# Reordered steps in a transformer kernel's second attention, and the spill slots' downward product joined with the next upward one

## The chip, the cores and the metric

The kernel runs on one core of one Trainium2 chip. The metric is the time on the device in microseconds (us), from the start of the launch to its end. A core has five engines that run side by side, each from a stream of instructions of its own: TensorE (PE in the profile, with its weight loads as PEld) multiplies matrices and transposes through an identity matrix, VectorE (DVE) works elementwise and along rows, ScalarE (ACT) applies functions such as the exponential, GpSimd (POOL) does general elementwise work and indirect transfers, and SyncE (SP) issues plain DMA transfers. An engine takes its instructions strictly in the order in which they were written to it; where one needs another engine's result, it waits on a semaphore, and everything behind it on that engine waits too. Matmul results go to PSUM, from which VectorE or ScalarE must copy them; operands of matmuls lie in SBUF.

## The reference

The input is `x [8, 256, 256]` (8 batches, 256 tokens, width 256) and a context of the same shape, in f32. Four residual stages follow one another, each on the layer norm of `x`:

```python
x = x + L0_xattn(layernorm(x), ctx, ctx)   # autocorrelation attention by FFT, top-12 shifts
x = x + L0_ffn(layernorm(x))               # 8 experts, balanced assignment, gelu
x = x + L1_xattn(layernorm(x), ctx)        # the attention of this document
x = x + L1_ffn(layernorm(x))               # the mixture of this document
```

The change touches the last two only. Cut to what matters:

```python
def L1_xattn(x, data):            # 16 heads of width 16
    q = (x @ Wq + bq).reshape(bs, n_ctx, 16, 16)
    kv = (data @ Wkv + bkv).reshape(bs, n_data, 16, 32)
    k, v = kv[..., :16], kv[..., 16:]
    attn = softmax(einsum('bqhd,bkhd->bhqk', q, k) / sqrt(16))
    return einsum('bhqk,bkhd->bqhd', attn, v).reshape(...) @ Wp + bp

def L1_ffn(x):                    # 8 routed experts, 8 shared slices
    probs = softmax(flat @ gate_W.T)
    top_v, top_i = top_k(probs, 2)           # two experts per token
    out_e = einsum('etf,efd->etd', silu(flat @ w1_e) * (flat @ w3_e), w2_e)
    routed = einsum('te,etd->td', gates, out_e)
    shared = einsum(..., silu(x @ w1_s) * (x @ w3_s), w2_s) / 8
    return 0.5 * shared + 0.5 * routed
```

## The kernel before

**Order.** The whole program is under a manual schedule: the order in which the Python code issues instructions is the order on each engine. Nothing plans or moves work afterwards. Work that is to overlap is therefore written between other work, with generators that are advanced step by step (`next`).

**Stages.** The first two residual stages end at some 217 us. The second attention runs from 217 to 349 us, the shared slices' first blocks around 349 to 397 us, and the blocks of the mixture to the end at 824 us.

**The attention** is a loop over 8 batches `b` and, inside, 2 halves `c` of 8 heads each (line 2968 onward). One iteration (b,c) issues, in this order: `scores(b,c,0)` for the first 128 keys (four matmuls that fill two PSUM tiles, then two exponentials `ex` on ScalarE; the pool of score tiles has two, so the next scores need both read); the values of the previous iteration (`values`, 16 matmuls with 32-wide weights) and their copy `ov` out of PSUM on VectorE (`keep`); one `send`; one step of the router; then a turning step that depends on c. With c = 0, `turn_q(b+1)` transposes the next batch's normalised tokens on TensorE into one PSUM tile and VectorE copies them to `hT`. With c = 1, `turn_out(b-1)` transposes the previous batch's attention output `on`, VectorE copies it to `oT`, and `norm_q(b+2)` with `add_bias(b+2)` normalise a later batch and add the output bias to it. Then come `scores(b,c,1)`, and behind them further router steps, the mixture's statistics for batch b-2 (`batch_stats` on VectorE and POOL, then `norm_m`, two normalisations on POOL that write into the row table `HP`), one more `send`, and the rest, by the half of the iteration: with c = 0 `turn_back` (transposes of `ov`, reciprocal sums `rs` and division into `on`), `queries(b+1, 0)` and `(b+1, 1)`; with c = 1 `turn_m` (mixture tokens transposed into `HT`), `project_out` (the product with Wp, added to X).

`queries` makes one PSUM tile `pp` of two matmuls and reads it twice into the masked `QM`: ScalarE writes the part m = 0, VectorE the part m = 1. These PSUM tiles, like those of the transposes and of the router, come from one pool, `ps_m`, with three buffers that go round in the order of allocation.

Batch 1 is an exception: in iteration (0,1) `turn_q(1)`, `norm_q(2)` and both `queries(1, ...)` all stand ahead of `scores(0,1,1)`. Batch 0 is another: ahead of the loop, `transpose_tokens` (line 1238) takes two PSUM tiles, one for each half of the width; VectorE copies the first and ScalarE the second.

**The router** (`route(g)`, for four tiles of 128 tokens, begun at b = 4 and b = 6) is a generator of eight steps: logits `pl` and their copy `lT`; their transpose `pt`, the row maximum and the exponential; two steps that pick the best and the second expert and end in the mask `mk`; the counting matmuls `pc` and the gates into `HP`; the running row numbers `run`, which read `pc`; the row numbers `to`. Each row tile is then sent by an indirect DMA of POOL (`send`) to the table `Td` in DRAM, ordered by expert.

**The mixture** works through 11 blocks: two of shared slices, eight experts (b = 2 to 9) and a last shared one. An expert's block is four upward units k = 0 to 3 and, between k = 0 and k = 1, the downward unit of the block before; a unit is a series of seven matrix products with 128-wide weights (recombined as in Strassen's method). Rows that an expert has above its fixed capacity go into four spill slots of 32 rows, whose experts are known only at run time. The generator `slots` handles them in quarters q of the hidden width, with the slots' weights loaded by SP at run-time addresses: `load_slots(q)` issues twelve DMAs of 256 KB (eight `sab` for w1 and w3, four `sc` for w2) into one buffer each. A quarter has three steps: up (`pgu`, 16 matmuls with 32-wide weights, then silu and product into `a`), turn (`a` transposed into `aT`), down (`pys`, 8 matmuls, 32 wide, followed by the loads of the next quarter). The block loop advances the generator by one step behind each unit k = 1 to 3. The quarters' steps stand at (3,1) to (6,3), so that one quarter goes with each of the blocks 3 to 6. The last step scales the sum into `Ys` and adds its rows to the output by indirect DMAs of POOL.

Of the kernel before, what the change touches and what calls it, by code (L numbers as in the profile page):

```python
# [19 lines left out]
P = 128  # L20
# [1066 lines left out]
def fast_path(  # L1087
# [1502 lines left out]
    def norm_q(b, *engs):  # L2590
        h2s[b] = hn.tile([P, TPB, D], F32, tag="h4", name="h2")
        batch_norm(b, "q", h2s[b], engs)
# [8 lines left out]
    def turn_pair(src, dst, copy):  # L2601
# [5 lines left out]
                )  # L2607
        copy(dst, pt.rearrange("p k j q -> p k (j q)"))

    def turn_q(b):  # L2610
        hTs[b] = pq2.tile([P, KC, S], F32, tag="hT", name="hT")
        turn_pair(h2s.pop(b), hTs[b], nc.vector.tensor_copy)

    def queries(b, c):
        if c == 0:
            QM[b] = pq2.tile([P, NB, 2, S], F32, tag="QM", name="QM")
        pp = ps_m.tile([P, S], F32, tag="pm", name="pp")
        for kc in range(KC):
            nc.tensor.matmul(  # L2619
                pp,  # L2620
                wq[:, kc, c * P : (c + 1) * P],
                hTs[b][:, kc, :],
                start=(kc == 0),
                stop=(kc == KC - 1),
            )
        nc.scalar.activation(
            QM[b][:, c, 0, :],
            pp,
            AF.Identity,
            bias=bqm[:, c, 0:1],  # L2630
            scale=mask[:, 0:1],
        )
        nc.vector.tensor_scalar(
            QM[b][:, c, 1, :],
            pp,
            mask[:, 1:2],
            bqm[:, c, 1:2],
            ALU.mult,
            ALU.add,
        )  # L2640

    pex = at.enter_context(tc.tile_pool(name="pex", bufs=4))
    ex, pvs, ovs, ons, oTs = {}, {}, {}, {}, {}
# [305 lines left out]
        list(vals(i, 2, ps_m))  # L2949
    norm_q(0, nc.vector, nc.vector)  # L2950
    hTs[0] = pq2.tile([P, KC, S], F32, tag="hT", name="hT")
    transpose_tokens(h2s[0], hTs[0], ps_m, "pm", 0)
    nc.vector.tensor_tensor(bpb, bpb, pbp, ALU.add)
    queries(0, 0)
    queries(0, 1)
# [12 lines left out]
    for b in range(B):  # L2968
        for c in range(NB):
            scores(b, c, 0)  # L2970
            if (b, c) == (3, 0):
                router_weights()
            if prev:
                values(*prev, 0)
                values(*prev, 1)
                keep(*prev)
            send()
            if gates:
                next(gates, None)
            if prev is None:  # L2980
                list(vals(4, 1, ps_m, nc.vector.tensor_copy))
            elif b == 0:
                turn_q(1)
                norm_q(2, nc.vector, nc.vector)
                queries(1, 0)
                queries(1, 1)
            elif c == 0:
                if b + 1 < B:
                    turn_q(b + 1)
            else:  # L2990
                turn_out(b - 1)
                if 2 < b + 2 < B:
                    norm_q(b + 2, nc.vector, nc.vector if b < 2 else nc.gpsimd)
                    add_bias(b + 2)
            scores(b, c, 1)
            if gates:
                next(gates, None)
            if c == 0 and b >= 2:
                batch_stats(b - 2, "m")
                norm_m(b - 2)  # L3000
            send()
            if gates:
                next(gates, None)
            if c == 0:
                if b >= 1:
                    turn_back(b - 1)
                if 0 < b and b + 1 < B:
                    queries(b + 1, 0)
                    queries(b + 1, 1)
                if b + 2 < B and b:  # L3010
                    add_y(b + 2)
                    batch_stats(b + 2, "q")
                if b >= 4 and b % 2 == 0:
                    gates = route(b // 2 - 2)
                    next(gates)
            else:
                if b >= 2:
                    turn_m(b - 2)
                if b >= 1:
                    project_out(b - 1)  # L3020
                else:
                    add_bias(2)
            if prev is None:
                list(vals(5, 1, ps_m, nc.vector.tensor_copy))
                ct_scope.close()
                wsp = ctx.enter_context(tc.tile_pool(name="wsp", bufs=1, side="right"))
                pg1 = ctx.enter_context(tc.tile_pool(name="pg1", bufs=1, side="right"))
# [12 lines left out]
                idx = pg1.tile([P, GT, E], F32, name="idx")  # L3040
                tri = pg1.tile([P, P], BF16, name="tri")
                ones_b = pg1.tile([P, P], BF16, name="ones_b")
                ends = pg1.tile([P, E], F32, name="ends")
                place_i = pg1.tile([P, 1], I32, name="place_i")
                slot = pg1.tile([P, 1], F32, name="slot")
                none = pg1.tile([P, 1], F32, name="none")
                bases = [
                    pg1.tile([P, E], F32, name=f"base{g}") for g in range(NT // GT + 1)
                ]
                nc.sync.dma_start(out=gw, in_=L1_ffn_gate_W)  # L3050
                WS = load_l1(wsp, -1)
            if (b, c) == (1, 0):
                router_columns()
            prev = b, c
# [4 lines left out]
    NQ = 4  # L3059
# [537 lines left out]
            for g in range(SLOTS)  # L3597
        ]

    def load_slots(q):  # L3600


        fs = slice(q * FQ, (q + 1) * FQ)
        wab = wsp.tile([P, 2, SLOTS, KC, FQ], F32, tag="wab", name=f"sab_{q}")
        wc = wsp.tile([P, SLOTS, FQ // P, D], F32, tag="wc", name=f"sc_{q}")
        wa, wb = wab[:, 0], wab[:, 1]
        for w, src in ((wa, L1_ffn_w1_e), (wb, L1_ffn_w3_e), (wc, L1_ffn_w2_e)):
            for g, e in enumerate(experts):
                part = src[bass.ds(e, 1)]
                part = part[:, fs, :] if w is wc else part[:, :, fs]  # L3610
                nc.sync.dma_start(
                    out=w[:, g], in_=part.rearrange("o (c p) d -> p (o c) d", p=P)
                )
        return wa, wb, wc

    def slots():

# [5 lines left out]
            in_=Td,  # L3623
            in_offset=bass.IndirectOffsetOnAxis(ap=rows_u, axis=0),
        )
        w = load_slots(0)
        yield
        gate = pg1.tile([P, 1], F32, name="gate")
        junk = pg1.tile([P, E], F32, name="junk")
# [14 lines left out]
        nc.vector.tensor_copy(RT, pt)  # L3644
        yield
        py = ps_v.tile([P, D], F32, tag="pv", name="pys")
        for q in range(NQ):
            pgu = ps_m.tile([P, 2, FQ], F32, tag="pm", name="pgu")
            for i in range(2):
                for kc in range(KC):  # L3650
                    for g in range(SLOTS):
                        nc.tensor.matmul(
                            pgu[g * SR : (g + 1) * SR, i, :],
                            RT[:, kc, g * SR : (g + 1) * SR],
                            w[i][:, g, kc, :],
                            start=(kc == 0),
                            stop=(kc == KC - 1),
                            skip_group_check=True,
                        )
            a = pe2.tile([P, FQ], F32, tag="as", name="as", bufs=1)  # L3660
            nc.scalar.activation(a, pgu[:, 0, :], AF.Silu)
            nc.vector.tensor_tensor(a, a, pgu[:, 1, :], ALU.mult)
            yield
            pt = ps_m.tile([P, FQ // P, P], F32, tag="pm", name="pt")
            for fi in range(FQ // P):
                nc.tensor.transpose(pt[:, fi, :], a[:, fi * P : (fi + 1) * P], ident)
# [3 lines left out]
            for fi in range(FQ // P):  # L3670
                for g in range(SLOTS):
                    nc.tensor.matmul(
                        py[g * SR : (g + 1) * SR, :],
                        aT[:, fi, g * SR : (g + 1) * SR],
                        w[2][:, g, fi, :],
                        start=(q == 0 and fi == 0),
                        stop=(q == NQ - 1 and fi == FQ // P - 1),
                        skip_group_check=True,
                    )
            if q + 1 < NQ:  # L3680
                w = load_slots(q + 1)
            else:
                WS = load_l1(wsp, -1)
                Y = pe2.tile([P, D], F32, tag="Ys", name="Ys", bufs=1)
                nc.scalar.activation(Y, py, AF.Copy, scale=gate)
                for g in range(SLOTS):
                    add_rows(Y[g * SR : (g + 1) * SR, :], ids[:, g : g + 1])
# [252 lines left out]
```

## Time and profile before

Three runs took 821.92, 823.33 and 821.46 us, a median of 821.92. One further execution was taken by the hardware profiler; it took 825.85 us, of which 824.1 lie between its first and its last instruction (its span).

| what | before |
|---|---|
| median of the runs | 821.92 us |
| profiled execution, whole | 825.85 us |
| profiled execution, span | 824.1 us |
| instructions | 13,790 |
| mean granted TensorE clock | 0.993 of full speed |
| HBM read, written | 80.61 MB, 25.37 MB |
| DMA mean | 133 GB/s |

TensorE's share by stage, with VectorE, ScalarE and POOL beside it (busy us):

| stretch, us | length | PE | DVE | ACT | POOL | clock |
|---|---|---|---|---|---|---|
| 0 to 217 | 217 | 204.34 | 121.05 | 87.52 | 64.43 | 0.98 |
| 217 to 349 | 132 | 126.45 | 82.28 | 81.20 | 60.55 | 0.99 |
| 349 to 397 | 48 | 48.00 | 25.60 | 12.82 | 20.01 | 1.00 |
| 397 to 824 | 427 | 419.83 | 290.36 | 180.21 | 71.61 | 1.00 |

How to read it: an instruction's line number (L2619) is that of the kernel printed above. A row of a chain or of the timeline gives the start in us from the span's start, the duration, the engine, and the written tile with its line. A row of windows gives, for a stretch, its length, then busy time and number of instructions of PE, PEld, DVE, ACT and POOL, the granted clock, the share of time in which the DMA engines were busy, and GB/s. Blocks 3 to 6, each with a quarter of the slots, take 40.16 us each; those without take 36.68.

### The profile page before, as it was taken

How to read it: one execution, taken by the hardware profiler on the slowest of the kernel's cores; microseconds unless marked ns; L12 is line 12 of the kernel's file. 1: busy time of each engine (PE TensorE's matmuls, PEld its weight loads, DVE VectorE, ACT ScalarE, POOL GpSimd, SP SyncE). 2: the span in 40 equal slices, each digit the busy share in tenths (PEclk: the TensorE clock that was granted, in tenths of full speed). 3: DMA queues.
4: the chain of work that ended last, by engine and by line, in shares of the span. 5: the costliest groups of instructions: out<-in, count | busy, mean ns of one | idle time of the engine just before them, and what ended most of it. 6: DMA issues, size and time to landing. Idle time of an engine off the chain costs nothing.

```text
span 824.1 us, 13790 instructions
## 1 busy us (share of the span) xinstructions
PE 798.6 (97%) x5124; PEld 630.4 (76%) x5124; DVE 519.3 (63%) x1470; ACT 361.8 (44%) x672; POOL 216.6 (26%) x293
## 2 busy tenths in 40 slices
PE   7999999999989999999999999999999999999997
PEld 6546778778745555556899989898979798999986
DVE  6368877440356585655685868676676768586731
ACT  4334544423356666532333544444444544443330
POOL 6343122131123646462330000202020323112030
PEclk9999999999999999999999999999999999999999
DMA  8395467962160100133214395385858495411023
GB/s 261 84 296 169 146 161 214 326 217 84 52 179 14 27 2 15 41 110 135 71 42 110 81 306 161 81 274 115 252 139 282 107 301 111 154 14 20 7 36 123
DMA packets 104724, 109.59 MB, mean 133 GB/s; under 512 B 26408, under 2 KB 95240, under 8 KB 104616
## 3 DMA queue, kind: packets, MB, share of 16 engines
q1 hardware_dynamic: 95976, 95.30, 38.1%
q0 software_dynamic: 7920, 13.02, 7.6%
q8 instruction: 42, 0.69, 0.4%
q10 hardware_dynamic: 752, 0.30, 0.1%
q14 instruction: 34, 0.28, 0.1%
HBM read 80.61 MB, written 25.37 MB: 129 GB/s over the span
## 4 chain that ended last, share of the span: by engine, by line
PE 88%; DVE 4%; DMA 4%; ACT 1%; issue 1%; POOL 0%; ACTq 0%; SPq 0%; DVEq 0%; POOLq 0%
PE a L3233 18%; PE e L3233 9%; PE a L3292 9%; PE py L2389 6%; PE ph L2372 6%; PE B L3233 5%; PE e L3292 4%; PE p L2652 4%; PE pv L2669 4%; PE pgu L3195 3%; PE py L3438 3%; PE B L3292 2%; DMA R<-NMd,ids 2%; PE pp L2720 2%; PE pp L2619 2%; PE pp L1419 2%
## 5 line engine op out<-in xcount | busy, mean ns | idle before, releaser
L3536 POOL DMA_INDIRECT Od<-Y,ids x32 | 52.3, 1636 | 288.1 <-DVE Y L3361 98.6
L3221 ACT COPY B<-a 128x512 f32<-128x512 f32 (+1 forms) x54 | 28.6, 531 | 169.6 <-PE a L3233 133.6
L2660 ACT ACTIVATE ex<-p,scale 128x1024 f32<-128x1024 f32 x64 | 67.9, 1111 | 34.1 <-PE p L2652 33.3
L3233 PE MATMUL a<-T,HP 128*128 128x256 f32 x288 | 73.9, 379 | 0.0
L3233 PE MATMUL a<-RT,wab 128*128 128x256 f32 x256 | 66.7, 383 | 0.4 <-DVE cc L3083 0.4
L3083 DVE TENSOR_TENSOR cc<-e,s 128x512 f32<-128x512 f32 x44 | 30.4, 691 | 57.6 <-PE e L3233 57.5
L2372 PE MATMUL ph<-RT,w 128*128 128x256 f32 x256 | 63.3, 396 | 0.8 <-ACT RT L2359 0.7
L3083 DVE TENSOR_TENSOR act<-act 128x256 f32<-128x256 f32 (+1 forms) x120 | 61.4, 512 | 2.7
L2389 PE MATMUL py<-w,A 128*128 128x256 f32 x256 | 61.6, 388 | 0.0
L3233 PEld LDWEIGHTS a<-T,HP 128*128 128x128 f32 x288 | 54.0, 190 | 7.0
L2381 ACT ACTIVATE A<-ph,b1c 128x256 f32<-128x256 f32 x64 | 30.1, 473 | 55.5 <-PE ph L2372 48.2
L2372 PEld LDWEIGHTS ph<-RT,w 128*128 128x128 f32 x256 | 46.3, 194 | 9.2 <-ACT A L2381 1.1
L3233 PEld LDWEIGHTS a<-RT,wab 128*128 128x128 f32 x256 | 46.3, 190 | 9.2 <-DVE cc L3083 2.5
L2389 PEld LDWEIGHTS py<-w,A 128*128 128x128 f32 x256 | 46.6, 190 | 6.4
L2894 POOL DMA_INDIRECT Td<-HP,to x32 | 33.0, 1030 | 60.5 <-DMA Td<-HP,to 52.6
L2652 PE MATMUL p<-QM,KT 32*128 32x512 f32 x256 | 40.5, 640 | 1.7 <-ACT ex L2660 1.2
L3083 DVE TENSOR_TENSOR act<-act,cc 128x512 f32<-128x512 f32 x44 | 30.3, 688 | 16.9 <-ACT act L3267 16.7
L2399 POOL DMA_INDIRECT Yd<-Y,ids x16 | 15.8, 986 | 83.3 <-DVE Y L2398 48.6
L3248 ACT COPY s<-a 128x512 f32<-128x512 f32 x44 | 25.8, 587 | 20.0 <-PE a L3233 20.0
L3233 PE MATMUL e<-T,wab 128*128 128x256 f32 x128 | 32.9, 380 | 0.3 <-DVE T L3083 0.3
L3233 PE MATMUL e<-RT,HP 128*128 128x256 f32 x128 | 32.8, 379 | 0.0
L3233 PE MATMUL B<-RT,wab 128*128 128x256 f32 x128 | 32.8, 379 | 0.0
(522 smaller groups left out, 1730.4 us busy)
## 6 DMA issues: line engine op xcount, KB each, us to landing
w<-in_L_ffn_w_dram SPq DMA_DIRECT2D x16, 1024.0 KB
wab<-in_L_ffn_w_e_dram SPq DMA_DIRECT2D x16, 1024.0 KB
wc<-in_L_ffn_w_e_dram SPq DMA_DIRECT2D x8, 1024.0 KB
sab<-in_L_ffn_w_e_dram SPq DMA_DIRECT2D x32, 256.0 KB
R<-Td SPq DMA_DIRECT2D x8, 530.0 KB
sc<-in_L_ffn_w_e_dram SPq DMA_DIRECT2D x16, 256.0 KB
Td<-blank SPq DMA_DIRECT2D x2, 1590.0 KB
X<-in_x_dram SPq DMA_DIRECT2D x4, 512.0 KB
```

Of the source, the lines that this page charges most:

```text
L2372: nc.tensor.matmul(ph, w1[:, kc, f * P : (f + 1) * P], RT[:, kc, :], start=(kc == 0), stop=(kc == KC - 1),)
L2381: nc.scalar.activation(A[:, f, :], ph, AF.Gelu_apprx_tanh, bias=b1c[:, e, f : f + 1])
L2389: nc.tensor.matmul(py, A[:, f, r * P : (r + 1) * P], w2[:, f, :], start=(f == 0), stop=(f == NF - 1),)
L2652: nc.tensor.matmul(ps[g // 2][:, g % 2].rearrange("p m q -> p (m q)"), KT[rows, c, k0 : k0 + P], QM[b][rows, c].rearrange("p m q -> p (m q)"),
L2660: nc.scalar.activation(e4[:, 2 * j : 2 * j + 2], ps[j], AF.Exp, scale=scale)
L2669: nc.tensor.matmul(pvs[b, c][32 * g : 32 * g + 32, m, :], VA[:, b * TPB + kt, 8 * c + 2 * g + m, :], ex[b, c, kt][:, g, m, :], start=(kt = ...
L2894: nc.gpsimd.indirect_dma_start(out=Td, out_offset=bass.IndirectOffsetOnAxis(ap=to[g][:, k, j : j + 1], axis=0), in_=HP[:, GT * g + j, :], ...
L3083: eng.tensor_tensor(out, a, b, op)
L3221: nc.scalar.copy(self.b[:, 0 : self.n], self.a[:, 0 : self.n])
L3233: nc.tensor.matmul(ps[:, m * HT2 : (m + 1) * HT2], self.w.get(m, left, self.k), self.x.part[right], start=start and m == 0, stop=True, ski ...
L3292: nc.tensor.matmul(ps[:, qs], self.acts[k][:, left, qs], self.w.get(right, k), start=start and i == 0 and k == 0, stop=(k == NK - 1), skip ...
L3536: nc.gpsimd.indirect_dma_start(out=Od, out_offset=bass.IndirectOffsetOnAxis(ap=ids, axis=0), in_=Y, in_offset=None, compute_op=ALU.add,)
```

## The change

It moves work between places of these two stages and changes the engine of two copies and of two masked products; the matmuls are the same in kind and number.

1. In iteration (0,1), both `queries(1, ...)` and `norm_q(2)` go from ahead of `scores(0,1,1)` to behind them (and behind the iteration's second `send`), the queries now ahead of `norm_q(2)`. For these queries both masked products are VectorE's (`eng=nc.vector`); for the other batches they stay split between ScalarE and VectorE.
2. Batch 0 is transposed by `turn_pair` into one PSUM tile, and two VectorE copies (`in_two`) take it to `hT`.
3. The mixture's statistics and `norm_m(b-2)` go from behind `scores(b,0,1)` to directly behind `scores(b,0,0)`, that is, ahead of the previous iteration's values, of `ov` and of `send`.
4. The first router step of an iteration goes behind `turn_q` or `turn_out`; `norm_q(b+2)` and `add_bias(b+2)` go behind that router step.
5. `load_slots` is split into upward and downward weights. A slots' step now holds the down product of quarter q and directly behind it the up product of quarter q+1; the turn stays a step of its own. The downward weights of q+1 are loaded behind the down product of q, the upward weights of q+2 behind the up product of q+1. The steps stand at (3,1) to (5,3): up 0; turn 0; down 0 and up 1; turn 1; down 1 and up 2; turn 2; down 2 and up 3; turn 3; down 3 with the additions.

```diff
+    def in_two(dst, src):
+        for kc in range(KC):
+            nc.vector.tensor_copy(dst[:, kc], src[:, kc])
+
-    def queries(b, c):
+    def queries(b, c, eng=nc.scalar):
...
+        for m in range(2):
+            if m == 0 and eng is nc.scalar:
+                nc.scalar.activation(
+                    QM[b][:, c, m, :],
+                    pp,
+                    AF.Identity,
+                    bias=bqm[:, c, m : m + 1],
+                    scale=mask[:, m : m + 1],
+                )
+            else:
+                nc.vector.tensor_scalar(
+                    QM[b][:, c, m, :],
+                    pp,
+                    mask[:, m : m + 1],
+                    bqm[:, c, m : m + 1],
+                    ALU.mult,
+                    ALU.add,
+                )
...
-    transpose_tokens(h2s[0], hTs[0], ps_m, "pm", 0)
+    turn_pair(h2s[0], hTs[0], in_two)
...
             scores(b, c, 0)
+            if c == 0 and b >= 2:
+                batch_stats(b - 2, "m")
+                norm_m(b - 2)
             if (b, c) == (3, 0):
                 router_weights()
...
             send()
-            if gates:
-                next(gates, None)
             if prev is None:
                 list(vals(4, 1, ps_m, nc.vector.tensor_copy))
             elif b == 0:
                 turn_q(1)
-                norm_q(2, nc.vector, nc.vector)
-                queries(1, 0)
-                queries(1, 1)
             elif c == 0:
                 if b + 1 < B:
                     turn_q(b + 1)
             else:
                 turn_out(b - 1)
-                if 2 < b + 2 < B:
-                    norm_q(b + 2, nc.vector, nc.vector if b < 2 else nc.gpsimd)
-                    add_bias(b + 2)
+            if gates:
+                next(gates, None)
+            if c == 1 and 2 < b + 2 < B:
+                norm_q(b + 2, nc.vector, nc.vector if b < 2 else nc.gpsimd)
+                add_bias(b + 2)
             scores(b, c, 1)
             if gates:
                 next(gates, None)
-            if c == 0 and b >= 2:
-                batch_stats(b - 2, "m")
-                norm_m(b - 2)
             send()
             if gates:
                 next(gates, None)
+            if (b, c) == (0, 1):
+                queries(1, 0, nc.vector)
+                queries(1, 1, nc.vector)
+                norm_q(2, nc.vector, nc.vector)
...
-    def load_slots(q):
...
+    def load_slots_up(q):
+        fs = slice(q * FQ, (q + 1) * FQ)
+        wab = wsp.tile([P, 2, SLOTS, KC, FQ], F32, tag="wab", name=f"sab_{q}")
...
+    def load_slots_down(q):
+        fs = slice(q * FQ, (q + 1) * FQ)
         wc = wsp.tile([P, SLOTS, FQ // P, D], F32, tag="wc", name=f"sc_{q}")
...
-        w = load_slots(0)
+        wab, wc = load_slots_up(0), load_slots_down(0)
         yield
...
-        for q in range(NQ):
+
+        def way_up():
             pgu = ps_m.tile([P, 2, FQ], F32, tag="pm", name="pgu")
...
-            yield
+            return a
+
+        a = way_up()
+        wab = load_slots_up(1)
+        yield
+        for q in range(NQ):
             pt = ps_m.tile([P, FQ // P, P], F32, tag="pm", name="pt")
...
             if q + 1 < NQ:
-                w = load_slots(q + 1)
+                wc = load_slots_down(q + 1)
+                a = way_up()
+                if q + 2 < NQ:
+                    wab = load_slots_up(q + 2)
             else:
                 WS = load_l1(wsp, -1)
```

More of the change, by code (lines that the diff above doesn't have):

```diff
@@ L2625, in queries @@
             )
[L2626 to L2640, printed above, removed]
+        for m in range(2):
[16 more added lines that the diff above has]
+                )
     pex = at.enter_context(tc.tile_pool(name="pex", bufs=4))
@@ L3598, in slot_experts @@
         ]
-    def load_slots(q):
+    def load_slots_up(q):
         fs = slice(q * FQ, (q + 1) * FQ)
         wab = wsp.tile([P, 2, SLOTS, KC, FQ], F32, tag="wab", name=f"sab_{q}")
-        wc = wsp.tile([P, SLOTS, FQ // P, D], F32, tag="wc", name=f"sc_{q}")
[L3606 to L3614, printed above, removed]
+        for m, src in enumerate((L1_ffn_w1_e, L1_ffn_w3_e)):
+            for g, e in enumerate(experts):
+                nc.sync.dma_start(
+                    out=wab[:, m, g],
+                    in_=src[bass.ds(e, 1)][:, :, fs].rearrange(
+                        "o (c p) d -> p (o c) d", p=P
+                    ),
+                )
+        return wab
+    def load_slots_down(q):
+        fs = slice(q * FQ, (q + 1) * FQ)
+        wc = wsp.tile([P, SLOTS, FQ // P, D], F32, tag="wc", name=f"sc_{q}")
+        for g, e in enumerate(experts):
+            nc.sync.dma_start(
+                out=wc[:, g],
+                in_=L1_ffn_w2_e[bass.ds(e, 1)][:, fs, :].rearrange(
+                    "o (c p) d -> p (o c) d", p=P
+                ),
+            )
+        return wc
     def slots():
@@ L3654, in slots @@
                             RT[:, kc, g * SR : (g + 1) * SR],
-                            w[i][:, g, kc, :],
+                            wab[:, i, g, kc, :],
                             start=(kc == 0),
@@ L3674, in slots @@
                         aT[:, fi, g * SR : (g + 1) * SR],
-                        w[2][:, g, fi, :],
+                        wc[:, g, fi, :],
                         start=(q == 0 and fi == 0),
```

## The prediction

> **What bounds the kernel now.** I read part 1 of the page first, then the chain that ended last, then that chain in order of time for the attention (217 to 349 us) and the mixture (349 to the end), and at last windows over the places where it leaves TensorE.
>
> ```profile
> PE 798.6 (97%) x5124; PEld 630.4 (76%) x5124; DVE 519.3 (63%) x1470; ACT 361.8 (44%) x672; POOL 216.6 (26%) x293
> PE 88%; DVE 4%; DMA 4%; ACT 1%; issue 1%; POOL 0%; ACTq 0%; SPq 0%; DVEq 0%; POOLq 0%
> ```
>
> TensorE is the path, so an edit pays only where PE idles, runs slow or pays for a change of shape. Over 470 us from 350 on, PE is busy 466.8, so only the attention has waits to give. In windows (us; then busy of PE, PEld, DVE, ACT, POOL; granted clock; DMA share; GB/s):
>
> ```profile
> 231.70:242.80 11.10, 9.08 (x72) 4.25 (x71) 6.28 (x14) 6.51 (x8) 5.24 (x8) 0.99 0.94 246
> 242.80:246.30 3.50, 3.50 (x35) 1.47 (x34) 0.00 (x0) 1.21 (x2) 0.00 (x0) 0.55 0.63 200
> 305.90:308.90 3.00, 1.14 (x15) 0.93 (x11) 2.66 (x14) 2.12 (x2) 1.06 (x3) 1.00 0.00 0
> ```
>
> PE loses 2.0 us before 242.8, then has half a clock, then loses 1.9 us in iteration (5,0), where VectorE is nearly full. From 246.3 to 305.9 it is busy all 59.6 us: what the change moves there is free unless it makes a wait. I write (b,c) for an iteration of the loop.
>
> **Part 1, queries of batch 1 behind the second scores of (0,1).** The chain there:
>
> ```profile
> 235.03 0.69 DVE ov L2679
> 235.72 0.61 DVE hT L2608
> ...
> 236.37 1.99 PE pp L2619 x8
> 238.37 1.08 PE p L2652 x8
> ...
> 239.47 1.12 ACT ex L2660
> ...
> 240.64 2.22 PE p L2652 x8
> 242.86 3.41 PE pv L2669 x32
> ```
>
> PE waits for hT, makes queries, then scores (p), and the next scores wait for an exponential (ex) that started late; as they wait for two, they run in halves, 2.22 us where a whole set takes 1.07. In the new order, step by step: transposes end 235.49; scores (0,1,1) follow at once, since both score tiles were free when ex of 232.92 ended at 235.04: to 236.56. Their ex runs 236.7 to 238.8. hT is there at 236.33, so queries 236.56 to 238.3. Both masked halves are now VectorE's: the first product starts 0.3 after its matmuls, 237.75, and c=0 is done after 2 x 0.544 (row QM L2633) at 238.85. Scores (1,0,0) start then, whole, as both ex ended at 238.8: to 239.97. The values start there and not at 242.86: **2.9 us**. norm_q(2), which held VectorE 1.73 beside POOL's add_bias, now stands behind the products, 239.95 to 240.7; its reader, turn_q(2), comes at 241.8. add_bias(2) on POOL waits for it; its X is needed two batches later. Bounds: 2.2 if the products start 0.7 later, 3.3 if PE has no wait left.
>
> **The clock.** In 242.5 to 245.9 the values ran at half clock, 3.41 for what takes 1.86 everywhere else: 1.55 us. [...] I take the row: 239.1 to 242.5 was busy well under two thirds, partly with 32-row matmuls; in the new order the longest gap there is 0.6. So 1.55 is saved in the profiled execution. [...]
>
> **Part 2, batch 0's transposes in one tile.** Before, the second pair of transposes waited for the copy of VA (0.46, until 223.32), and ACT's copy of hT ended 224.30. Now four transposes run 222.49 to 223.1 and VectorE copies both halves, 0.42 each. [...] Bounds 0 and 0.55. bpb's addition comes behind the copies at 224.0 and has until 225.1.
>
> **Part 3, mixture's statistics behind the first scores.** Five VectorE instructions, 1.4 us in a row (306.24 to 307.6), go ahead of ov, POOL's reciprocal root (0.71) and two normalisations (2.44) with them. At b=2 VectorE idles 2.68 before ov, at b=6 and 7 some 1.9: free. At b=3 the router's weights stand there too (about 1.5 us): ov starts 0.6 late and hT ends 276.85; the reader is queries at 277.4, still covered; were it not, up to 0.6. One send per iteration from b=6 on stands behind the normalisation; the chain of sends is paced by its own landings (2.8 each, to 432.4), its load of R(0) is issued at 434.2, read at 443.7: covered.
>
> **Part 4, router steps behind the copies, with part 3 at (5,0).**
>
> ```profile
> 305.62 0.60 DVE hT L2608
> 306.22 0.10 DVE HP L2855
> 306.32 0.35 DVE b_st L2562
> ...
> 308.56 0.20 DVE run L2868
> ...
> 308.90 1.98 PE pp L2619 x8
> ```
>
> Queries need the bank that `run` frees, and `run` stands behind the statistics. New order: X 302.57, statistics to 304.6, ov 305.2, hT 305.9, picks and mk (0.6) 306.5. **A wait is added**: PE's pc matmul, ready at 305.9, waits 0.65 for mk, with the transposes of ov (1.07) queued behind it, to 307.63. HP and `run` (1.35) end 307.87; queries start 307.9: 1.0 gained. At (5,1) oT stands ahead of the 1.15 us of rows and PE's 0.30 wait at 316.05 goes. Its gain is then 1.4. At (7,1) the same 0.24 wait (345.0) goes. At (4,1) and (6,1) lg comes within 0.1 of ACT's next exponential: nothing. **Sum 1.6**, bounds 0.7 (mk 0.5 later, oT's wait stays) and 2.0.
>
> **Part 5, slots.** Matmuls unchanged; what falls is the change between 128-wide and 32-wide weights. Timeline of PE, the last quarter step:
>
> ```profile
> 534.03 1.03 PE L3233 MATMUL a<-T,HP 128*128 128x256 f32 x4
> 534.98 1.07 PE L3672 MATMUL pys<-sc,aT 128*32 128x256 f32 x16
> 535.99 1.13 PE L3233 MATMUL a<-RT,wab 128*128 128x256 f32 x4
> ```
>
> A group of four elsewhere starts 0.86 after the last; here 0.95 before pys and 0.96 after it: about 0.1 at each border. Three joins save two borders each: **0.6 us** (0.4 to 0.8). Each block with a quarter lasts 40.16 against 36.68; the sum of quarters moves from four blocks into three.
>
> The loads are the danger. Load of up 1 is issued when the first quarter's up is done, 522.6, over 5.4 us of SP (eight issues at 539.48 took that), and is read at (3,3) behind pys, 535.9. 2 MB at the 309 GB/s of 540 to 560, beside a DMA share of 0.23 in 523 to 536, is some 8.5 us: landed by about 532 (an estimate from these rows), 4 us early. What queues behind on SP: the four transposes of (3,3) (534.1), not held. At (4,2) three quarters of a block's issues go ahead of the transposes of (4,3): SP is free at 575.7, they were issued at 574.2; their reader on ACT is at 587 before, about 589 now: covered. wab, R and wc of the following blocks come no later than before. On POOL the slots' four additions now precede a block's four, at most 5 us late; Y is rewritten 10 us after. Price at nothing; if late, each us is a us.
>
> **Sum.** 2.9 + 1.55 + 0.3 + 1.6 + 0.6 = 6.95 us of the profiled execution (span 824.1, whole 825.85), which makes 817.15 and 818.9. The median of the runs is 821.92, 3.9 below the profiled time; with half of the clock, 6.2 off: **815.7 us**. Less than 0.2% (1.6 us) can't be told from no change.
>
> **Rivals.**
> A, the waits move (0.15): the products on VectorE start late and scores (1,0,0) run in halves after all (+1.07 and 0.6: 1.2 left of 2.9), the clock stays, mk's wait eats part 4 to 0.7. 0.3 + 1.2 + 0.7 + 0.6 = 2.8: **819.1**. For it: VectorE is the full engine in both places. Against: in 231.7 to 242.8 it is busy 6.28 of 11.1.
> B, slower (0.07): load of up 1 comes late to (3,3). The stall decides once it exceeds 6.2 us, that is landing after 542.1, under 2 MB in 18 us, 116 GB/s. At 100 GB/s it lands near 544, 8 us late: **823.9**. For it: POOL's accumulating writes hold a DMA share of 0.93 at 526 with 96 GB/s. Against: they hold it 2 us in 5, and loads elsewhere ran at 295 and 309 GB/s.
> C, all upper bounds with the clock in the median (0.10): 3.3 + 1.55 + 0.55 + 2.0 + 0.8 = 8.2: **813.7**.
> That PE does fewer matmuls is none: their number is the same.
>
> **Numbers.** Main case 0.68, its own range 814.2 to 818.6 (lower bounds without the clock, 2.2 + 0 + 0.7 + 0.4 = 3.3, to nearly the upper). For 8 in 10: 813.5 to 819.3. Faster: main, C and two thirds of A, 0.88; within 0.2%: the rest of A, 0.05; slower: B, 0.07.
>
> **What would show it.** Values (0,1) start some 8.2 us after scores (0,1,0), not 11.1, and take 1.9; clock 1.00 throughout. At (5,0) pc waits for mk, and queries start about 1 us earlier against the scores before. Between pys and pgu no PEld gap; the pair starts behind (3,3) without one. Wrong if PE waits for DMA at the first pair, if p at (1,0) takes over 2 us, or if ov at b=3 delays queries.

## The result: 5.9 us less, and the profile after

Over 14 runs of each kernel, the changed one takes 816.38 us (814.07 to 822.47) and the one before 822.27 us (820.63 to 827.92). The ratio is 0.9927, with a 95% interval of 0.9908 to 0.9947. The profiled execution took 814.97 us with a span of 812.8. From the page, the rows of busy time and the shares of the chain that ended last:

```profile
PE 790.3 (97%) x5124; PEld 628.8 (77%) x5124; DVE 520.4 (64%) x1473; ACT 359.7 (44%) x669; POOL 215.0 (26%) x293
...
PE 89%; DMA 4%; DVE 4%; ACT 1%; issue 1%; POOL 1%; SPq 0%; DVEq 0%; ACTq 0%; POOLq 0%
```

TensorE still bounds the kernel with the same 5,124 matmuls, yet its busy time fell from 798.6 to 790.3. A busy row can hold half a clock (in the kernel before, the values at 242.86 took 3.41 us, where 1.86 is usual) or a group that runs slower behind a wait (1.99 against 1.89 us at (5,1), shown below), so I compared where each group of matmuls starts. The start of the values in every iteration is a good ruler: between two profiles these distances repeat within 0.02 us unless something was changed or the clock was halved. There is one exception, 0.13 us at (6,1) in the first profile of the kernel before, whose cause was not traced. In the changed kernel, the place that was before the worst (chain of waits, iteration (0,1)) reads:

```profile
231.66 0.59 PE pt L2605 x4
232.24 1.08 PE p L2659 x8
...
233.35 2.13 ACT ex L2667 x2
...
235.56 1.14 PE p L2659 x8
236.70 1.86 PE pv L2676 x32
```

The second scores follow the transposes at once, the next ones (235.56) run whole, and the values take 1.86 us. The wait for hT and the run in halves are gone. One wait is left: the scores at 235.56 wait 0.32 us for the second exponential, which ends at 235.47.

The whole difference between the two profiled executions, by start against start:

| place | predicted gain, us | measured gain, us |
|---|---|---|
| ahead of 216 us, code that was not changed | 0 | 3.36 |
| part 2, batch 0's transposes | 0.3 | -0.06 |
| part 1 at (0,1), waits and half a clock | 2.9 + 1.55 | 4.40 |
| (2,0), (3,0), (4,0), (6,0) | 0 | 0.37 |
| (5,0) | 1.0 | 0.98 |
| (5,1) | 0.4 | 0.56 |
| (6,1) | 0 | 0.13 |
| (7,1) | 0.2 | 0.50 |
| part 5, blocks of the mixture | 0.6 | 1.00 |
| sum | 6.95 | 11.24 |

(The 0.13 at (6,1) is missing in a second pair of profiles; it belongs to no step of the change. The spans differ by 11.3 us, so 0.1 us lies outside these rows.)

The first row is luck. The execution before had half a clock at 41 and at 102 us, some 1.6 us each; that of the changed kernel had none there. It had one at 11 us, which cost nothing: its matmuls were 0.32 us ahead of those of the kernel before at 10 us and 0.54 ahead at 16 us. What the luck consists in is shown in the last section.

### The profile page after: what moved, and what is told of

The parts are those of the page before. It is cut to its first block, busy times and chain, and to the rows that moved or that the text cites. A ratio compares the mean times of both kernels' runs of the same rounds, so it can differ in the third digit from the quotient of the medians.

```text
span 812.8 us, 13791 instructions
## 1 busy us (share of the span) xinstructions
PE 790.3 (97%) x5124; PEld 628.8 (77%) x5124; DVE 520.4 (64%) x1473; ACT 359.7 (44%) x669; POOL 215.0 (26%) x293
## 4 chain that ended last, share of the span: by engine, by line
PE 89%; DMA 4%; DVE 4%; ACT 1%; issue 1%; POOL 1%; SPq 0%; DVEq 0%; ACTq 0%; POOLq 0%
PE a L3241 19%; PE e L3241 9%; PE a L3300 9%; PE py L2389 7%; PE ph L2372 6%; PE B L3241 5%; PE e L3300 4%; PE p L2659 4%; PE pgu L3203 3%; PE pv L2676 3%; PE py L3446 3%; PE B L3300 2%; DMA R<-NMd,ids 2%; PE pp L1419 2%; PE pp L2727 2%; PE pp L2623 1%
```

## The experiments

Each kernel is the changed one with one edit, unless it says otherwise. Dots in a diff stand for lines that are not shown. With one part undone, the interval of each ratio overlaps that of the changed kernel, so the parts are read from the starts in the profiles and not from the medians.

### Part 1 undone, and its engine alone

```diff
                 turn_q(1)
+                norm_q(2, nc.vector, nc.vector)
+                queries(1, 0)
+                queries(1, 1)
...
-            if (b, c) == (0, 1):
-                queries(1, 0, nc.vector)
-                queries(1, 1, nc.vector)
-                norm_q(2, nc.vector, nc.vector)
```

> The changed kernel with part 1 alone undone (queries and norm_q(2) ahead of scores (0,1,1), one masked product on ScalarE). Theory (the waits for hT and for the late exponential were the cost): the values of (0,1) start 9.8 us behind those of (0,0) again, against 6.9 in the changed kernel and 9.76 before, so about 2.9 us more; all other distances between values stay within 0.1. On the clock, my theory is that the thin stretch before 242 lets TensorE's clock be halved in some executions, for about 1.55 us more; if it is halved at this place in this profile the theory gains, if not it is left open. Rival (the two profiles differ by luck of the clock in code that wasn't changed): less than 1 us comes back at this place. Time by the theory: 2.5 to 4.5 us above the changed kernel; by the rival under 1.

The values of (0,1) started 9.67 us behind those of (0,0), against 6.91 in the changed kernel: 2.76 us came back, and no other distance moved by more than 0.02. The median was 819.88 us, 0.9959 of the kernel before beside it (0.994 to 0.9979). The clock was not halved there. So the waits are worth 2.76 us.

The other half of part 1 is the engine of the first masked product:

```diff
-                queries(1, 0, nc.vector)
-                queries(1, 1, nc.vector)
+                queries(1, 0)
+                queries(1, 1)
```

> The changed kernel with the first masked product of batch 1 on ScalarE instead of VectorE (the place stays behind the second scores). Theory: ScalarE is held by the two exponentials of scores (0,1,1) until 235.47, so the product starts only then, VectorE's half behind it, and scores (1,0,0) start at 236.6 to 236.8 instead of 235.56: the values of (0,1) come 0.9 to 1.3 us later against those of (0,0). Rival (the place alone is worth the 2.85, the engine nothing): less than 0.3 us later.

The values came 0.99 us later. The chain of waits shows why:

```profile
238.36 2.12 ACT ex L2667 x2
240.48 0.47 ACT QM L2632
...
240.97 0.56 DVE QM L2640
...
241.57 1.14 PE p L2659 x8
```

ScalarE reaches the product only behind two exponentials, and VectorE's half stands behind ScalarE's. The new place alone is worth 1.77 of the 2.76 us; the engine gives the rest. (The median was 820.86 us, 0.9961 of the kernel before, 0.9931 to 0.9991; the profile has another wait of 0.5 us, of the kind described below with the sends.)

### The kernel before, and the changed one, once more

> The kernel before once more, for a second profile of it. My prediction put 1.55 us of half a clock at 242 down to the thin stretch of TensorE's work there. If it is halved again within 236 to 250, the stretch causes it; if it is not, it depends on more than the stretch (in the changed kernel with part 1 undone, which has the same stretch, it wasn't halved) and belongs to no sum of the change. All distances between values as in the first profile within 0.05 us, but for stretches with half a clock.

> The changed kernel once more, on the chip of the next runs, for a second profile of it. Theory (the distances between the values are set by the order of work alone): each of them as in the first profile, within 0.05 us, outside of stretches with half a clock. [...]

The kernel before was halved again in the same place. In windows of 3.41 us (columns as in the prediction), with the stretch ahead of the halved one first:

```profile
236.04:239.45 3.41, 2.39 (x16) 0.84 (x20) 0.00 (x0) 3.13 (x4) 0.00 (x0) 1.00 1.17 308
239.45:242.86 3.41, 3.41 (x34) 1.54 (x27) 0.31 (x1) 0.96 (x1) 0.00 (x0) 0.50 0.55 173
```

TensorE was busy 2.39 of 3.41 us (70%), then ran a whole stretch at 0.50. Over this place both profiles of the kernel before are 4.40 us longer than the changed kernel; the waits alone are 2.76, which leaves 1.64 for half a clock. In the kernel with part 1 undone the same thin stretch was not followed by half a clock:

```profile
237.90:241.30 3.40, 2.20 (x14) 0.67 (x12) 0.69 (x2) 2.62 (x4) 0.72 (x1) 1.00 1.21 293
241.30:244.70 3.40, 3.40 (x44) 1.55 (x45) 0.63 (x2) 2.06 (x2) 0.00 (x0) 1.00 0.88 280
```

It was thinner (65%) and yet spared. So with the queries in their old place two of three profiles were halved there, and with them in the new place none of eleven. The busy share of the thin stretch does not settle it: 65% and 70% were followed by half a clock, another 65% was not. What decides here is left open.

The changed kernel's second profile has all distances of the first within 0.02 us. It has half a clock at 40 and 102 us, as the first profile of the kernel before had. Set side by side, these two tell the change without the first row of the table: spans of 824.1 and 816.0, 8.1 us apart, of which 1.64 is the halved stretch at 242. The median of ten runs was 818.56 us beside 824.34 us of the kernel before, ratio 0.9947 (0.9915 to 0.9979).

### Parts 3 and 4, each undone

Part 3 first: the statistics stand behind the second scores again.

```diff
             scores(b, c, 0)
-            if c == 0 and b >= 2:
-                batch_stats(b - 2, "m")
-                norm_m(b - 2)
...
             scores(b, c, 1)
             if gates:
                 next(gates, None)
+            if c == 0 and b >= 2:
+                batch_stats(b - 2, "m")
+                norm_m(b - 2)
             send()
```

> The changed kernel with part 3 alone undone (mixture's statistics behind the second scores again). Theory: the 1.28 us of statistics ahead of the running row numbers carried the gain at (5,0), and the router's new place cost a little there: the step of 0.98 us at (5,0) is given back, whole or nearly (0.8 to 1.1), while the gains of 0.56 at (5,1) and 0.50 at (7,1) stay within 0.1. Rival (the router's new place carried (5,0)): less than 0.3 us comes back at (5,0). Time by the theory about 1 us above the changed kernel, by the rival no difference.

At (5,0) 2.73 us came back, far more than expected. TensorE's timeline says why; the wait in brackets is the idle row ahead of the group:

```profile
298.18 0.18 PE L2859 MATMUL pc<-mk,ones_b 128*128 128x32 bf16 x1 [0.30 <-DVE mk L2855]
...
298.23 1.08 PE L2696 MATMUL pt<-ident,ov 128*128 128x128 f32 x8
300.94 3.49 PE L2623 MATMUL pp<-hT,wq 128*128 128x256 f32 x8 [1.62 <-DVE run L2875]
```

The same place in the changed kernel:

```profile
298.45 0.18 PE L2859 MATMUL pc<-mk,ones_b 128*128 128x32 bf16 x1 [0.46 <-DVE mk L2855]
...
298.50 1.07 PE L2696 MATMUL pt<-ident,ov 128*128 128x128 f32 x8
299.93 1.97 PE L2623 MATMUL pp<-hT,wq 128*128 128x256 f32 x8 [0.35 <-DVE run L2875]
```

With part 3 undone the waits are 1.92 us against 0.81, which is 1.1 more. The rest is mostly half a clock: the granted clock was 0.50 from 301.2 to 304.6, and the queries take 3.49 where they take 1.97 in the changed kernel, behind a stretch of 3.4 us in which TensorE was busy 1.48. So the statistics carried (5,0), as the theory said. The gains at (5,1) and (7,1) stayed; the 0.09 at each of (2,0), (3,0), (4,0) and (6,0) went, and (6,1) lost 0.49, a wait that neither the kernel before nor the changed one has and that was not traced. Part 3 gives 0.37 us besides what it gives at (5,0). The median was 820.07 us, ratio 0.9962 (0.9939 to 0.9986).

Part 4 undone puts the first router step ahead of the turning again:

```diff
             send()
+            if gates:
+                next(gates, None)
             if prev is None:
...
                 turn_out(b - 1)
-            if gates:
-                next(gates, None)
```

> The changed kernel with part 4 alone undone (first router step of an iteration ahead of turn_q or turn_out, norm_q and add_bias right behind turn_out). Theory: VectorE is serial at (5,0), so there nothing changes in sum (within 0.2 us; the wait of the counting matmul goes, that of the queries grows), while 0.56 at (5,1) and 0.50 at (7,1) come back, together some 1.0 us. Rival (the two parts share (5,0)): 0.4 us or more comes back at (5,0) too, 1.5 us in all. Second rival: the gains at (5,1) and (7,1) come from the statistics, and nothing comes back.

At (5,1) 0.55 came back, at (7,1) 0.47, and (5,0) became 0.10 shorter. At these three places the parts divide cleanly: the statistics made (5,0), the router's place made the other two. The timeline at (5,1), with part 4 undone:

```profile
309.56 0.66 PE L2605 MATMUL pt<-ident,HP 128*128 128x128 f32 x4
310.52 1.99 PE L2727 MATMUL pp<-wp,oT 128*128 128x256 f32 x8 [0.30 <-DVE oT L2721]
312.44 1.14 PE L2659 MATMUL p<-QM,KT 32*128 32x512 f32 x8
```

and in the changed kernel:

```profile
306.42 0.66 PE L2605 MATMUL pt<-ident,HP 128*128 128x128 f32 x4
306.91 1.89 PE L2727 MATMUL pp<-wp,oT 128*128 128x256 f32 x8
308.73 1.15 PE L2659 MATMUL p<-QM,KT 32*128 32x512 f32 x8
```

From start to start it is 0.96 + 1.92 = 2.88 us with the wait and 0.49 + 1.82 = 2.31 without. The idle row says 0.30, the wait costs 0.57: without it, the next group starts 0.17 ahead of the end of the last, and it also runs 0.10 faster. The median was 818.28 us, ratio 0.9937 (0.9919 to 0.9955).

### Part 5 undone, and its load made late

> The changed kernel with part 5 alone undone (slots in three steps a quarter). Theory (each border between 128-wide and 32-wide weights costs 0.1 ahead of it and some 0.2 behind it, so a join saves 0.33): the four blocks with a quarter last 40.16 us each again, 1.0 us more in all than in the changed kernel. Rival (only 0.1 at a border, as in the prediction): 0.6 us. Second rival (the later steps of the slots only move the cost): nothing. The time of a run can't tell these apart, the starts of the blocks in the profile can.

The edit takes `load_slots` and `slots` of the kernel before. Between the same two groups of the first and the last block it was 270.68 us, against 269.68: 1.00 us, and the four blocks took 40.16 each again. The changed kernel at a join:

```profile
524.73 1.07 PE L3695 MATMUL pys<-sc,aT 128*32 128x256 f32 x16
525.62 1.91 PE L3670 MATMUL pgu<-sab,RTs 128*32 128x256 f32 x32
```

The up product starts 0.89 behind the down product; before, the next 128-wide group started 1.01 behind it (534.98 to 535.99 in the prediction's lines). That is 0.12. An up product that stands alone also starts 0.96 behind the group ahead of it, and the second group behind a narrow product starts 0.97 behind the first, where wide groups follow each other at 0.86. A join saves one of each, 0.33 us in all. The median, 818.71 us (ratio 0.9957, 0.9939 to 0.9975), can't show one us.

To see how near the danger was, one load was made longer:

```diff
-        wab = load_slots_up(1)
+        wab = load_slots_up(1, 2)
...
-        for m, src in enumerate((L1_ffn_w1_e, L1_ffn_w3_e)):
+        for m, src in list(enumerate((L1_ffn_w1_e, L1_ffn_w3_e))) * times:
```

> The changed kernel with the load of the slots' second upward weights issued twice into the same buffer: eight DMAs more, nothing else. Theory (in the changed kernel this load lands some 2.8 us ahead of its first reader, so it is hidden, but narrowly): eight more issues move the last landing back by 5 to 6 us, and the joined up product of (3,3) waits 2 to 4 us, which go into the time whole. Rival (the load is far ahead, as the estimate of my prediction had it, 4 us or more): it waits under 2 us.

```profile
529.93 0.92 PE L3670 MATMUL pgu<-sab,RTs 128*32 128x256 f32 x6
531.09 1.05 PE L3670 MATMUL pgu<-sab,RTs 128*32 128x256 f32 x10 [0.24 <-DMA sab<-in_L_ffn_w_e_dram]
532.65 0.62 PE L3670 MATMUL pgu<-sab,RTs 128*32 128x256 f32 x2 [0.51 <-DMA sab<-in_L_ffn_w_e_dram]
533.54 1.33 PE L3670 MATMUL pgu<-sab,RTs 128*32 128x256 f32 x4 [0.27 <-DMA sab<-in_L_ffn_w_e_dram]
535.09 1.05 PE L3670 MATMUL pgu<-sab,RTs 128*32 128x256 f32 x10 [0.22 <-DMA sab<-in_L_ffn_w_e_dram]
```

The up product is taken apart by the landings; the block became 4.29 us longer (46.18 against 41.89), a little above the range of the theory. The idle rows sum to 1.24 us: here too they understate the loss. In the changed kernel this load's last issue is at 516.9, and the two landings of it that the profile holds took 5.4 and 5.9 us. By that it is there at 522.8, 2.8 us ahead of its reader; the DMA rate agrees, as it falls from 225 GB/s (512.5 to 522.5) to 12 (522.5 to 523.0).

### Part 2 undone

```diff
-    turn_pair(h2s[0], hTs[0], in_two)
+    transpose_tokens(h2s[0], hTs[0], ps_m, "pm", 0)
```

> The changed kernel with part 2 alone undone (batch 0 transposed into two tiles, one copied by VectorE and one by ScalarE). From the start of the bias matmuls (pbp) to the first scores it was 8.11 us before and 8.17 in the changed kernel. Theory (the copies in turn on VectorE from one tile cost what the missing wait saves): 8.11 within 0.05, so nothing comes back. Rival (the 0.3 us of my prediction, hidden by something else in the change): 8.4 or more.

It was 8.11 us, in one profile, as in both profiles of the kernel before; the changed kernel has 8.17 in both of its own. Part 2 brings nothing and costs 0.06.

### Two versions beyond the changed kernel

At (5,0) two waits are left, 0.46 for `mk` and 0.35 for `run`. The first edit covers them with the turning of batch 4's output:

```diff
             scores(b, c, 1)
+            if (b, c) == (5, 0):
+                turn_back(b - 1)
             if gates:
...
-                if b >= 1:
+                if b >= 1 and b != 5:
                     turn_back(b - 1)
```

> The changed kernel with the turning of batch 4's output (turn_back) put ahead of the counting matmuls at (5,0), to cover both waits left there (0.46 for the mask, 0.35 for the running numbers). Theory (the queries of batch 6 then wait for the division that frees the first turned tile, not for the running row numbers, and the counting matmuls stand behind 1 us of transposes): 0.5 to 0.9 us less at (5,0), all else the same. Rival (VectorE is serial there, so what the queries wait for only changes its name): within 0.2 us, or later by up to 0.5 as reciprocal and division now go ahead of the running numbers.

It gained 0.45 us at (5,0), just under the theory's range; the queries now wait 0.42 for the division. But in its profile 5.8 us were lost at 360. POOL's timeline:

```profile
350.46 0.97 POOL L2901 DMA_INDIRECT Td<-HP,to  x1 [1.90 <-DMA Td<-HP,to]
355.08 0.97 POOL L2901 DMA_INDIRECT Td<-HP,to  x1 [3.65 <-DMA Td<-HP,to]
360.62 0.97 POOL L2901 DMA_INDIRECT Td<-HP,to  x1 [4.57 <-DMA Td<-HP,to]
...
363.58 2.43 POOL L2581 TENSOR_SCALAR HP<-X,b_mv,b_r 128x256 f32<-128x256 f32 x2
```

Four sends stand ahead of the last batch's statistics on POOL. Each waits for the landing of the one before, mostly some 1.9 us, here 3.65 and 4.57. From the start of batch 7's projection to the normalisation it was 10.9 us (352.64 to 363.58), against 6.2 in the changed kernel (351.38 to 357.56), so it came 4.8 us late; TensorE waited 2.96 and 0.88 us for it, and half a clock followed (the eight products at 366.45 took 5.30 us, against 3.60 in the changed kernel). This need not come from the edit: among the twelve profiles with the sends in this place, four have such a wait of 0.5 us or more. The second edit puts two of the four sends behind the normalisation:

```diff
     norm_m(B - 2)
-    send(4)
+    send(2)
...
     norm_m(B - 1)
+    send(2)
```

> The changed kernel with four sends behind the loop split: two stay ahead of the last batch's statistics, two go behind its normalisation (norm_m(7)). In four of the ten profiles so far a send waited 2.8 to 4.0 us for the landing of the one before instead of some 1.9, the normalisation queued behind it on POOL came late, and TensorE waited 0.5 to 3.8 us for it, in two of them followed by half a clock. Theory (this late normalisation makes a good part of the spread between runs): no wait of TensorE for POOL around 360 us in this profile, and a median 0.5 to 1.5 us below the changed kernel's beside it, with fewer runs far above it. Rival 1 (the spread comes from the clock in the first stages): same median within 0.5, same spread. Rival 2 (the sends end later and the first expert's rows with them): a new wait for these rows near 430 us, slower by 1 to 4 us.

> The split sends and the turning ahead of the counting matmuls at (5,0) together, on the changed kernel. Theory: 0.45 us less at (5,0), as in the profile with that edit alone, no wait for POOL around 360 us; in all 1 to 2 us below the changed kernel, 0.98 to 0.99 of the kernel before. Rival (the spread comes from elsewhere): 0.45 us below the changed kernel, not to be told from it by the runs.

In both profiles the wait is gone, and the 0.45 at (5,0) is there in the second. Medians of six runs were 815.46 us and 814.94 us, ratios 0.9920 (0.9899 to 0.9940) and 0.9924 (0.9902 to 0.9947), highest runs 816.39 and 817.37. The intervals overlap that of the changed kernel: by time the versions can't be told from it, and the gain of 1 to 2 us that was expected of both edits together isn't shown. That they have fewer runs far above the median fits the theory, but six runs don't show it. A new wait for rows near 430 us did not come.

## Why the prediction was right, and where it was off

The median was forecast at 815.7 us and was 816.38; the change of the median was forecast at 6.2 and was 5.9. That lies in the main case's own range, 814.2 to 818.6. The signs of the main steps were right, but errors of opposite sign meet in the sum, so that it came within 0.3 us is in part luck. Rivals A and B did not come: the scores (1,0,0) ran whole, against A, and the load of up 1 was there 2.8 us early, against B. Part 4 and part 5 even came out above the upper bounds of C, 2.04 us at the three places against 2.0 and 1.00 against 0.8.

- **Part 1** held step by step: the scores (1,0,0) were forecast 3.36 us behind the second scores (235.49 to 238.85) and came 3.32 behind them (232.24 to 235.56); the waits gave 2.76 where 2.9 was forecast. The undone kernel and the one with ScalarE show that place and engine are both needed.
- **The clock**: 1.55 was forecast for the profile and 1.64 came. The row was rightly taken for the profile: both profiles of the kernel before ran the values at half clock there, and no profile with the queries in the new place did. Yet the reason given was too strong. The stretch before 242.5 was busy 65%, not well under two thirds, and at (5,0) the prediction's own row has 1.14 of 3.00, and full clock behind it. The forecast takes half of the clock, 0.8 us, off the median; no run shows that term. The steps of the table without this clock and without the first row sum to 6.2 us, already above the 5.9 of the median. The interval of the ratio leaves 4.4 to 7.6 us for the change, so the medians can't tell whether a term of 0.8 is in it.
- **Part 2** was the step with the wrong sign, though small: no run shows the 0.3 us of the sum or the bound of 0.55, and the starts gave -0.06 in their place. The first copy started at 219.83, behind all four transposes (219.12 to 219.72), and the second ended at about 220.6, as forecast (224.0 less the 3.36 of the first row). What I left out is that before, half of the first query's matmuls had run while the second copy was awaited, 0.71 us were left behind it (224.34 to 225.05). In the changed kernel the first of the four starts only at 220.51, when the second copy is nearly done, and they take 1.12. The saved copy time is paid back there. Of that start, 0.25 us behind the first copy is a gap for which the profile shows no cause.
- **Part 3** was priced at nothing outside (5,0) because the windows show TensorE busy throughout, and gave 0.37 in four iterations. At (2,0) the 0.09 lies inside the busy row: the eight matmuls of the queries take 1.98 us before, 1.99 with part 3 undone and 1.89 in the changed kernel. What held them isn't shown.
- **Part 4 with 3**: the mechanism at (5,0) was right (0.98 for 1.0), with the added wait for `mk` at 0.46 instead of 0.65. The step that was mis-sized is the price of the waits at (5,1) and (7,1): "PE's 0.30 wait" and "the same 0.24" were read from the idle row (the sum then takes 0.4 for the first, without a reason), and cost 0.56 and 0.50.
- **Part 5**: "about 0.1 at each border" counted the start ahead of a narrow product and the second start behind it. It left out the first start behind it, which is 0.12 later than in a join. A join gives 0.33 and not 0.2. The load was on time; of the 4 us forecast as slack 2.8 were there, and the doubled load shows that being late would have cost whole.

## What to carry to other kernels

Price a wait, or a border between shapes, by the distance from start to start of the groups around it in a place with and one without it, not by the idle row: here 0.30 of idle cost 0.57 us. Where an engine is full, look at what stands ahead of the instruction that another engine waits for: here moving 1.3 us of statistics ahead of that chain, to where VectorE still had room, took 1.1 us of waiting from TensorE. Undo moved steps one at a time to learn which of them made the gain. When two profiles differ by more than the change explains, look where the granted clock was halved before giving the difference to the change: here 3.36 of 11.3 us were not the change's.

## What the runs showed of the hardware

Half a clock came in stretches of 3.41 us: in the fourteen profiles of this study there are 22 inside the work, each one such stretch long but for one of two (366 to 373 us with part 3 undone). All began directly behind a stretch of that length in which TensorE, by its rows, was busy only 31 to 76%, with no gap over 2.4 us: in the first profile of the kernel before 75, 56 and 65% ahead of the three halvings at 41.17, 102.61 and 242.56, in that of the changed kernel 41% ahead of the one at 10.93. The reverse does not hold: in the first profile of the kernel before, 307.4 to 310.8 (56%, at (5,0)) was not followed by one. The thin stretch at (0,1) thus cost another 1.64 us in both profiles of the kernel before, and nothing in that with part 1 undone.

Near 102 us the profiles show what the luck consists in. In the first profile of the kernel before, the three halvings lie 61.44 and 139.95 us apart, 18 and 41 times 3.413. Counted in steps of 3.413 us from the halved ones, such stretches begin at other places of the work in another execution: ahead of 102 us at 99.20 in the kernel before, and at 96.26 and 99.67 in the changed one. The thin place near 98 us, which is the same in all, is thus divided differently: the thinnest of these stretches is busy 56 to 62% in the six profiles that were halved there (56% in the first of the kernel before), and 64 to 77% in the eight that were not (66% in the first of the changed kernel). The two nearest to the border are the kernel with part 2 undone, which was halved, and that with part 3 undone, which was not:

```profile
97.37:100.78 3.41, 2.10 (x25) 1.66 (x26) 2.54 (x13) 1.02 (x2) 0.98 (x1) 1.00 0.64 192
100.78:104.19 3.41, 3.41 (x12) 2.11 (x10) 1.65 (x7) 1.43 (x3) 0.47 (x1) 0.50 0.69 235
...
96.41:99.82 3.41, 2.19 (x26) 1.54 (x24) 3.20 (x16) 0.44 (x2) 0.61 (x1) 1.00 0.38 96
99.82:103.23 3.41, 3.11 (x16) 2.34 (x17) 2.25 (x14) 2.13 (x5) 0.37 (x1) 1.00 1.08 351
```

This border was seen at that place alone. Between places with other matmuls the busy share didn't decide: 56% at (5,0) was spared, and 75% ahead of 41.17 us in the same profile, or 76% at 37 us in the kernel with part 4 undone, was not.

Besides, a send's landing is not steady. The same indirect DMA took POOL some 1.9 us of waiting in most cases and 2.8 to 4.6 in others, 5.3 (5.26 and 5.24) beside the loads of the first expert in the versions with split sends. Other traffic is not the whole cause: of the two slow ones in POOL's timeline above, that of 4.57 us stood at a DMA share of 0.96, that of 3.65 at 0.14.
